# Turning x by VectorE's 32x32 squares and transfers, and loading mixing's x behind its store

## The chip, the cores and the metric

The kernel runs on one core of a Trainium2 chip. The metric is the device time of one execution in microseconds. Every engine of the core (TensorE for matmuls, VectorE, ScalarE and GpSimd for the rest, SyncE for starting transfers) has its own queue of instructions and works through it in order. They wait for each other by semaphores.

## The reference

A graph network of four layers works on x of 8 batches, 2048 nodes and 64 features. Each layer adds its result to x and normalizes over the features.

```python
# layer 0: hypergraph attention; "industry" and "g" are mixed with two weights per node
industry = einsum('nm,bmf->bnf', adj / deg, x @ W_ind)
g        = einsum('bne,benf->bnf', coefs1, all_he)
coefs2   = softmax(attn_scores(stack([industry, g], 2)), -1)      # "mixing"
x = layernorm(x + einsum('bnk,bnkf->bnf', coefs2, pair))
# layer 1: x = layernorm(x + (A_hat @ x) @ W.T)
# layer 2: supports I, adj, 2*adj@adj - I, softmax(relu(E @ E.T)); weights per node
x_g = einsum('knm,bmc->bknc', supports, x)
out = einsum('bnki,nkio->bno', x_g, einsum('nd,dkio->nkio', emb, weights_pool)) + bias
# layer 3: three steps of v -> W2 @ relu(W1 @ [v, adj @ v] + b1) + b2
for _ in range(3):
    h = relu(einsum('bnk,dk->bnd', concat([v, adj @ v]), W1) + b1)
    v = einsum('bnk,dk->bnd', h, W2) + b2
```

## The kernel before

Batches are handled in pairs (p = 0 to 3), so that two batches' 64 features fill 128 partitions. The nodes lie in 16 tiles of 128, or in 4 chunks (c) of 512. adj stays in SBUF. The big products (`u`) go through TensorE in the order of the program. A "filler" generator supplies their matmuls between other work; `fill(n)` takes n of them. After each of them `tick()` counts down what `later(n, f)` and `after(n, f)` have put off. The list of `later` is served strictly in its order: an entry that is due waits for those ahead of it. On the other engines a scheduler decides the order of most instructions when the kernel is built; those wrapped in `pin` keep the order of the program.

Mixing of step i (pair and chunk) loads g, turns it for TensorE, loads x into `r` (two buffers) and adds g to it on GpSimd:

```python
def mix_g(i):
    p, c = divmod(i, NCH)
    gn = mp.tile([P, JT, P], F32, tag="gn", name="gn", bufs=2)
    nc.sync.dma_start(gn, gs_hbm...)                      # cut
    rs[i] = mp.tile([P, JT, P], F32, tag="r", name="r", bufs=2)
    load_x(rs[i], p, c)
    pg = lps.tile([P, C], F32, tag="mm", name="pg", bufs=4)
    for j in range(JT):
        transpose(pg[:, cols(j, P)], gn[:, j, :])
    gts[i] = mp.tile([P, C], F32, tag="gt", name="gt", bufs=2)
    pin(nc.scalar.activation(gts[i], pg, AF.Identity, bias=-1.0))
    r = rs[i]
    after(8, lambda: pin(nc.gpsimd.tensor_tensor(r, r, gn, ALU.add)))

def mix_scores(i):
    # cut: four matmuls pf, four tanh on ScalarE
    pin(nc.gpsimd.tensor_tensor(inds[i], inds[i], gts[i], ALU.subtract))
    after(5, differences)

def mix_end(i):
    # cut: pt <- transposes of inds[i]
    def end():
        nc.sync.dma_start(x1_hbm[p][:, wide(c), :], r)    # frees the buffer r
        # cut
    after(3, add_up, 0, *normalized(mp, r, r, False, end))

for i in range(steps + 1):
    k = 9 if i > NCH else 8
    if i < steps:
        mix_scores(i); fill(k)
    if i > 0:
        mix_end(i - 1); fill(k)
    if i + 1 < steps:
        mix_load(i + 2); mix_ind(i + 1); mix_g(i + 1); fill(k)
    if i < steps:
        mix_weigh(i); fill(k)
```

Layer 2 needs x turned (features on the partitions) in DRAM, to be loaded as a part of `xg`. Each chunk is turned while u1 = adj @ x is made:

```python
def out_t(hbm, c, src, eng):
    ut = va.tile([P, C], F32, tag="ut", name="ut", bufs=2)
    # cut: copy src (PSUM) to ut by ScalarE or VectorE
    nc.sync.dma_start(hbm[:, cols(c)], ut)

def natural(c, ut):
    pn = lps.tile([P, JT, P], F32, tag="mm", name="pn", bufs=4)
    for j in range(JT):
        transpose(pn[:, j, :], ut[:, cols(j, P)])
    x_part[c] = split(va, pn, f"v{c}", 1, [P, JT, P])

def turned_x(p, c):
    pt = lps.tile([P, C], F32, tag="mm", name="pt", bufs=4)
    for j in range(JT):
        transpose(pt[:, cols(j, P)], xn[p][:, c * JT + j, :])
    out_t(xt_hbm[p], c, pt, nc.scalar)
    # cut: xn += bias on GpSimd

# in supports(): k = 1 is u1 = adj @ x, k = 2 is u2 = adj @ u1, each in two halves g
if k == 1 and g == 0:
    turned_x(p, q)                       # after each chunk q of the first half
if k == 1 and g == 1 and q in uts:
    natural(q, uts.pop(q))               # u1 of the first half, turned back for k = 2

def load_xg(p, c, b):
    until(p, 2, c // 2)
    a, z = (l2.tile([P, C], F32, tag=f"g{2 * b + q}", name=f"xg{b}{q}") for q in range(2))
    # cut: four transfers from xt_hbm, u1_hbm, u2_hbm, u3_hbm into halves of a and z
```

Layer 2's products with the weights (`py`) follow for each pair and chunk, with `fill(2)` between them; VectorE multiplies each by the embeddings and sums it up. Layer 3 needs x turned in SBUF, as `h`:

```python
def first_h(p, c, h):
    pt = lps.tile([P, C], F32, tag="mm", name="pt", bufs=4)
    for j in range(JT):
        transpose(pt[:, cols(j, P)], xn[p][:, c * JT + j, :])
    nc.scalar.copy(h, pt)
    if c == 0:
        nc.vector.tensor_copy(h[:, 0:1], ivc)
    return h

def first(c, n):
    h[c] = first_h(0, c, l2.tile([P, C], F32, tag=f"g{c}", name=f"h{c}"))
    later(n, lambda: factor(c, h[c], bd_e, None))   # factor: matmuls pr, then the split into v0h, v0l, ...

# layer 3, for each pair p, step and half g (cut)
if last and p + 1 < NP:
    for c in own:
        def prepare(c=c):
            h_next[c] = first_h(p + 1, c, new_h(c))
        later(2 if g else 40, prepare)
# ... in g == 1 of the last step: later(3, factor(c, h_next[c], ...)) for c = 0 to 2, and c = 3 at its end
# ... and of the half before: later(14 + 8 * k, finish(p, c, h)): po, layernorm, out_x <- r
```

A `check` at several t of each half loads a piece of adj into `fcav` and compares it.

Of the kernel before, what the change touches and what calls it, by code (L numbers as in the profile page):

```python
# [30 lines left out]
F32 = mybir.dt.float32  # L31
# [6 lines left out]
ALU = mybir.AluOpType  # L38
# [18 lines left out]
def tile_gnn_fast(  # L57
# [265 lines left out]
    def products():  # L323

        deg1 = hy.tile([P, NT], F32, name="deg1")

        def degrees(g):
            du = pph.tile([P, 2, C], F32, tag="ph", name=f"du{g}", bufs=2)
            for t in range(NT):
                for i in range(2):  # L330
                    mm(
                        du[:, i, :], lhsT=ones_r, rhs=adj_c(t, 2 * g + i), start=t == 0, stop=t == NT - 1
                    )
                    yield
            for i in range(2):
                c = 2 * g + i
                r = slice(c * P // NCH, (c + 1) * P // NCH)
                evacuate(deg4[r, :], du[r, i, :])

        def inverses():  # L340

            pdc = places["small"]([P, JT, P], "pdc")
            for j in range(JT):
                transpose(pdc[:, j, :], deg4[:, cols(j, P)])
            pdc = pdc.rearrange("p j (c r) -> p c j r", c=NCH)[:, :, :, 0]
            d1 = deg1.rearrange("p (c j) -> p c j", c=NCH)
            nc.vector.tensor_scalar(d1, pdc, 1.0, None, op0=ALU.add)
            nc.gpsimd.tensor_tensor(dinv, deg1, neg_half[:, :NT], ALU.pow)
            nc.vector.tensor_scalar(d1, pdc, 1.0, None, op0=ALU.max)
            nc.vector.reciprocal(deg1, deg1)  # L350
            for _ in range(8):
                yield
            for c in range(NCH):
                pt = places["small"]([P, C], "pinv")
                for j in range(JT):
                    k = c * JT + j
                    transpose(pt[:, cols(j, P)], deg1[:, k:k + 1].to_broadcast([P, P]))
                row = va.tile([P, C], F32, tag="ut", name="inv", bufs=2)
                nc.scalar.copy(row, pt)
                nc.sync.dma_start(inv_hbm[:, cols(c)], row)  # L360
                for _ in range(4):
                    yield

        for p in range(NP):
            for g in range(2):
                own = (2 * g, 2 * g + 1)
                ug = pph.tile([P, 2, C], F32, tag="ph", name="ug", bufs=2)
                u = {c: ug[:, c % 2, :] for c in own}
                turning = inverses() if p == 0 and g == 1 else iter(())
                for t in range(NT):  # L370
                    for i in range(2):
                        for c in own:
                            mm(
                                u[c], lhsT=part[t // JT][i][:, t % JT, :], rhs=adj_c(t, c),
                                start=t == 0 and i == 0, stop=t == NT - 1 and i == 1,
                            )
                            tick()
                            if t > 1:
                                next(turning, None)
                            yield  # L380
                    if p == NP - 1 and g == 1 and t % JT == JT - 1:
                        first_parts(t // JT, free)
                    if p + 1 < NP and t % JT == JT - 1:
                        c = t // JT
                        if g == 1:
                            parts(p + 1, c)
                        if g == 1 and c < 2 or g == 0 and c >= 2:
                            fetch(p + 1, (c + 2) % NCH)
                if p == NP - 1:

                    for t in range(g * NT // 2, (g + 1) * NT // 2):
                        onto_diagonal(t, nc.gpsimd, ALU.add)
                for c in own:
                    ut = va.tile([P, C], F32, tag="ut", name="ut", bufs=2)
                    nc.scalar.copy(ut, u[c])
                    nc.sync.dma_start(u0_hbm[p][:, cols(c)], ut)
                if p == 0 and g == 0:
                    yield from degrees(0)
                    yield from degrees(1)
# [412 lines left out]
    def wide(c):  # L812
        return slice(c * JT, (c + 1) * JT)

    uts, invs, gts, inds, tts, rs = {}, {}, {}, {}, {}, {}
    xn, done, stored, due = [], [0] * NP, set(), set()


# [49 lines left out]
# [4 lines that stand above are left out]
        nc.sync.dma_start(  # L872
            gn, gs_hbm.rearrange("(p t) f -> p t f", t=NT)[:, wide(c), p * P:(p + 1) * P]
        )
        rs[i] = mp.tile([P, JT, P], F32, tag="r", name="r", bufs=2)
        load_x(rs[i], p, c)
        pg = lps.tile([P, C], F32, tag="mm", name="pg", bufs=4)
        for j in range(JT):
            transpose(pg[:, cols(j, P)], gn[:, j, :])
        gts[i] = mp.tile([P, C], F32, tag="gt", name="gt", bufs=2)  # L880
        pin(nc.scalar.activation(gts[i], pg, AF.Identity, bias=-1.0))
        r = rs[i]
        after(8, lambda: pin(nc.gpsimd.tensor_tensor(r, r, gn, ALU.add)))

    def mix_scores(i):

        t1 = []
        for src in (inds[i], gts[i]):
            for b in range(2):

                s = slice(b * F, (b + 1) * F)
                pf = lps.tile([P, C], F32, tag="mm", name="pf", bufs=4)
                mm(pf, lhsT=fc2[s, :], rhs=src[s, :], start=True, stop=True)
                t1.append(mp.tile([P, C], F32, tag="t1", name="t1", bufs=4))
                pin(nc.scalar.activation(t1[-1], pf, AF.Tanh, bias=fcb_col))
        tts[i] = t1[0:2]

        def differences():
            for b in range(2):
                pin(nc.vector.tensor_tensor(t1[b], t1[b], t1[2 + b], ALU.subtract))  # L900

        pin(nc.gpsimd.tensor_tensor(inds[i], inds[i], gts[i], ALU.subtract))
        after(5, differences)

    def mix_weigh(i):

# [10 lines left out]
    def mix_end(i):  # L917
        p, c = divmod(i, NCH)
        r = rs.pop(i)
        pt = lps.tile([P, C], F32, tag="mm", name="pt", bufs=4)  # L920
        for j in range(JT):
            transpose(pt[:, cols(j, P)], inds[i][:, cols(j, P)])

        def end():
            nc.sync.dma_start(x1_hbm[p][:, wide(c), :], r)
            stored.add((p, c))
            if p == 0:
                first_parts(c, mixed)
            elif (p, c) in due:
                l1_parts(p, c)  # L930

        def add_up():
            pin(nc.vector.scalar_tensor_tensor(
                r, pt.rearrange("p (t f) -> p t f", f=P), 0.5, r, op0=ALU.mult, op1=ALU.add
            ))

        after(3, add_up, 0, *normalized(mp, r, r, False, end))
# [85 lines left out]
    mix_load(1)  # L1023
    fill(24)
    mix_ind(0)
    fill(12)
    mix_g(0)
    fill(4)
    for i in range(steps + 1):
        k = 9 if i > NCH else 8  # L1030
# [162 lines left out]
    def natural(c, ut):  # L1193
# [3 lines left out]
            transpose(pn[:, j, :], ut[:, cols(j, P)])  # L1197
        x_part[c] = split(va, pn, f"v{c}", 1, [P, JT, P])

    def turned_x(p, c):  # L1200
        pt = lps.tile([P, C], F32, tag="mm", name="pt", bufs=4)
        for j in range(JT):
            transpose(pt[:, cols(j, P)], xn[p][:, c * JT + j, :])
        out_t(xt_hbm[p], c, pt, nc.scalar)

        bias = l2.tile([P, JT, 1, F], F32, tag="bias", name="bias", bufs=1)
        nc.sync.dma_start(bias[:, :, 0, :], bias_hbm[:, wide(c), :])
        x4 = xn[p][:, wide(c), :].rearrange("p t (b f) -> p t b f", f=F)
        nc.gpsimd.tensor_tensor(x4, x4, bias.to_broadcast([P, JT, 2, F]), ALU.add)
# [88 lines left out]

    def first_h(p, c, h):

        pt = lps.tile([P, C], F32, tag="mm", name="pt", bufs=4)
        for j in range(JT):
            transpose(pt[:, cols(j, P)], xn[p][:, c * JT + j, :])
        nc.scalar.copy(h, pt)
        if c == 0:

            nc.vector.tensor_copy(h[:, 0:1], ivc)
        return h
# [21 lines left out]
    for p in range(NP):  # L1330
        for c in range(NCH):
            r = staged("r").rearrange("p t (b f) -> p t b f", f=F)
            for b in range(2):
                a_z = xg[b]
                for j in range(JT):
                    e_b = emb_n[:, c * JT + j:c * JT + j + 1, :].to_broadcast([P, OH, D])
                    for k in range(2):
# [5 lines left out]
                        nc.vector.tensor_tensor(pr, py, e_b, ALU.mult)  # L1343
                        nc.vector.tensor_reduce(r[:, j, b, cols(k, OH)], pr, AX.X, ALU.add)  # L1344
                        fill(2)
                    if p == NP - 1 and c == NCH - 1 and b == 1 and j in (1, 2):

                        first(j - 1, 2)
                if c + 1 < NCH:
                    load_xg(p, c + 1, b)  # L1350
                elif p + 1 < NP:
# [9 lines left out]

    STEPS = 3
    for c in (2, 3):
        first(c, 4 * c)
    bd_v2 = l2.tile([P, P], F32, name="bd_v2")
    rows = l2.tile([P, 2, P], F32, tag="e", name="rows")
    more = l2.tile([P, 2, P], F32, tag="bias", name="more")
# [888 lines left out]
```

## Time and profile before

| | |
|---|---|
| time, median of 3 runs | 1966.11 us (1965.88 to 1972.42) |
| span of the profiled execution | 1961.8 us |
| mixing | about 240 to 500 us |
| softmax support of layer 2 (`ua`) | about 546 to 786 us |
| supports and weights of layer 2 | about 786 to 1482 us |
| layer 3 | about 1483 to 1962 us |
| `pt<-ident,xn` | 128 transposes, 789.7 to 1819.8 us, 272 ns each from start to end |
| `r<-in_x_n` | 16 transfers of 256 KB, 2.7 us to landing |
| VectorE, ScalarE, GpSimd busy | 51%, 20%, 27% |

The page has the busy time of each engine, the chain of work that ended last, and the groups of instructions; the trace can be asked for the waits of one engine and for stretches of time. PE is TensorE, PEld its loads of weights, DVE VectorE, ACT ScalarE, POOL GpSimd, SPq SyncE's queue, in which transfers are issued. In `pt<-ident,xn` the name before the arrow is written and those behind it are read. Matmuls overlap, so what one costs is read from the distance between starts and not from its duration.

### The profile page before, as it was taken

How to read it: one execution, taken by the hardware profiler on the slowest of the kernel's cores; microseconds unless marked ns; L12 is line 12 of the kernel's file. 1: busy time of each engine (PE TensorE's matmuls, PEld its weight loads, DVE VectorE, ACT ScalarE, POOL GpSimd, SP SyncE). 2: the span in 40 equal slices, each digit the busy share in tenths (PEclk: the TensorE clock that was granted, in tenths of full speed). 3: DMA queues.
4: the chain of work that ended last, by engine and by line, in shares of the span. 5: the costliest groups of instructions: out<-in, count | busy, mean ns of one | idle time of the engine just before them, and what ended most of it. 6: DMA issues, size and time to landing. Idle time of an engine off the chain costs nothing.

```text
span 1961.8 us, 19565 instructions
## 1 busy us (share of the span) xinstructions
PE 1867.9 (95%) x7100; PEld 1211.1 (62%) x7100; DVE 1004.3 (51%) x1741; ACT 392.7 (20%) x771; POOL 529.5 (27%) x480
## 2 busy tenths in 40 slices
PE   6888899888899999999999999999999999999997
PEld 4666565555754444855665575566547787877875
DVE  7789555565532211356556736754785343343332
ACT  1455343333222121100000000000002121222211
POOL 3678644454454434311001101100001020100201
PEclk9999899999999999999999999999999999999999
DMA  9923333432500000311101111111111122121211
GB/s 322 308 87 107 121 129 126 127 118 80 175 6 27 25 3 22 119 38 60 48 33 43 57 52 33 46 57 35 43 33 35 43 55 54 44 54 49 54 27 24
DMA packets 94185, 143.10 MB, mean 73 GB/s; under 512 B 29232, under 2 KB 40112, under 8 KB 93696
## 3 DMA queue, kind: packets, MB, share of 16 engines
q1 hardware_dynamic: 83920, 105.39, 17.7%
q0 software_dynamic: 7760, 27.66, 4.2%
q10 hardware_dynamic: 2400, 8.72, 1.2%
q8 instruction: 58, 0.95, 0.2%
q14 instruction: 47, 0.39, 0.1%
HBM read 98.67 MB, written 43.06 MB: 72 GB/s over the span
## 4 chain that ended last, share of the span: by engine, by line
PE 76%; DMA 4%; POOL 3%; DVE 3%; issue 2%; ACT 1%; SPq 0%; POOLq 0%; ACTq 0%; DVEq 0%
PE u L171 34%; PE py L171 22%; PE ua L171 11%; PE pr L171 2%; PE ug L171 2%; POOL ln_r L843 1%; DMA x_hbm<-r 1%; PE po L171 1%; DMA r<-in_x_n 1%; PE pf L171 1%; PE pt L174 1%; PE s L171 1%; DVE r L846 0%; DMA gs_hbm<-acc,order 0%; POOL r L968 0%
## 5 line engine op out<-in xcount | busy, mean ns | idle before, releaser
L171 PE MATMUL py<-wp,xg 128*128 128x512 f32 x1024 | 475.2, 592 | 0.7 <-DMA xg<-u_hbm 0.7
L171 PEld LDWEIGHTS py<-wp,xg 128*128 128x128 f32 x1024 | 193.3, 189 | 161.4 <-issue 138.8
L1343 DVE TENSOR_TENSOR fcav<-py,emb_n 128x512 f32<-128x512 f32 x256 | 176.9, 691 | 135.0 <-PE py L171 129.1
L171 PE MATMUL ua<-pt,xn 128*128 128x512 f32 x512 | 230.2, 592 | 1.5 <-DVE pt L1124 1.5
L1344 DVE TENSOR_REDUCE r<-fcav 128x32 f32<-128x512 f32 x256 | 175.5, 686 | 8.2
L171 PEld LDWEIGHTS ua<-pt,xn 128*128 128x128 f32 x512 | 96.9, 190 | 111.2 <-issue 104.2
L154 POOL TENSOR_TENSOR ln_r<-ln_e,neg_half 128x8 f32<-128x8 f32 x32 | 53.5, 1671 | 399.4 <-DVE ln_e L152 370.0
L171 PE MATMUL u<-adj,v0h 128*128 128x512 f32 x384 | 147.7, 452 | 1.3 <-ACT h L1499 1.3
L171 PE MATMUL u<-adj,v2l 128*128 128x512 f32 x384 | 141.0, 432 | 1.3 <-DVE v2l L167 1.3
L171 PE MATMUL u<-adj,v2h 128*128 128x512 f32 x384 | 141.3, 434 | 0.0
L171 PE MATMUL u<-adj,v1h 128*128 128x512 f32 x384 | 140.8, 434 | 0.0
L171 PE MATMUL u<-adj,v0l 128*128 128x512 f32 x384 | 139.8, 431 | 0.0
L171 PE MATMUL u<-adj,v3l 128*128 128x512 f32 x384 | 138.9, 426 | 0.0
L171 PE MATMUL u<-adj,v1l 128*128 128x512 f32 x384 | 138.4, 427 | 0.0
L171 PE MATMUL u<-adj,v3h 128*128 128x512 f32 x384 | 138.4, 427 | 0.0
L1124 DVE TENSOR_SCALAR pt<-pt 128x512 f32<-128x512 f32 x64 | 30.3, 473 | 150.5 <-ACT pt L1123 150.3
L1130 POOL TENSOR_TENSOR acc<-acc,pt 128x512 f32<-128x512 f32 x60 | 76.5, 1275 | 107.0 <-DVE pt L1124 106.4
L1425 DVE SCALAR_TENSOR_TENSOR ar<-fcav,ar 128x512 f32<-128x512 f32 x64 | 46.8, 731 | 108.7 <-ACT ar L1424 108.7
L171 PEld LDWEIGHTS u<-adj,v0h 128*128 128x128 f32 x384 | 71.0, 189 | 36.7 <-issue 24.1
L171 PEld LDWEIGHTS u<-adj,v2l 128*128 128x128 f32 x384 | 72.8, 191 | 31.9 <-issue 15.9
L171 PEld LDWEIGHTS u<-adj,v1l 128*128 128x128 f32 x384 | 72.9, 190 | 29.3 <-issue 14.4
L171 PEld LDWEIGHTS u<-adj,v3l 128*128 128x128 f32 x384 | 72.1, 188 | 29.4 <-issue 14.9
(360 smaller groups left out, 2717.2 us busy)
## 6 DMA issues: line engine op xcount, KB each, us to landing
adj<-in_adj_t POOLq DMA_DIRECT2D x32, 512.0 KB, 8.0
fcav<-in_adj_t SPq DMA_DIRECT2D x64, 256.0 KB, 2.9
u_hbm<-ut SPq DMA_DIRECT2D x48, 256.0 KB, 2.8
xg<-u_hbm SPq DMA_DIRECT2D x96, 128.0 KB, 2.9
x_hbm<-r SPq DMA_DIRECT2D x28, 256.0 KB, 2.2
hs_hbm<-st ACTq DMA_DIRECT2D x8, 584.0 KB, 5.4
xt<-in_x_t SPq DMA_DIRECT2D x16, 256.0 KB, 6.1
ut<-u_hbm SPq DMA_DIRECT2D x16, 256.0 KB, 3.4
```

The lines of the kernel that those rows point to most:

```text
L154: nc.gpsimd.tensor_tensor(rstd, vare, neg_half[:, :groups], ALU.pow)
L171: tc.keep_in_program_order(nc.tensor.matmul(*args, **kw))
L174: tc.keep_in_program_order(nc.tensor.transpose(dst, src, ident))
L843: pin(nc.gpsimd.tensor_tensor(rstd, vare, neg_half[:, :groups], ALU.pow))
L1124: nc.vector.tensor_scalar(pt, pt, 1.0, None, op0=ALU.max)
L1130: nc.gpsimd.tensor_tensor(accs[c], accs[c], pt, ALU.add)
L1343: nc.vector.tensor_tensor(pr, py, e_b, ALU.mult)
L1344: nc.vector.tensor_reduce(r[:, j, b, cols(k, OH)], pr, AX.X, ALU.add)
L1425: nc.vector.scalar_tensor_tensor(ar.bitcast(F32), seen_a, 1.0, ar.bitcast(F32), op0=ALU.mult, op1=ALU.not_equal, accum_out=left[:, t, k:k ...
```

## The change

Two things are changed. First, x of layers 2 and 3 is no longer turned by TensorE: VectorE transposes the 32x32 squares of a 128x512 tile, each in its place, and 16 transfers carry the squares to where they belong, to DRAM in layer 2 and to SBUF in layer 3. It is meant to take the transposes and their evacuations from TensorE, PSUM and ScalarE. The distances of `first` are set anew for it. Second, mixing's x is asked for behind the store that frees its buffer, and g is added to it later in the step, behind ind - gt, so that GpSimd should not stand waiting. The rows of inverse degrees are turned some matmuls later.

```diff
@@ inverses
-            for _ in range(8):
+            for _ in range(20):
                 yield
@@ mix_g
-        rs[i] = mp.tile([P, JT, P], F32, tag="r", name="r", bufs=2)
-        load_x(rs[i], p, c)
+        gns[i] = gn
...
-        r = rs[i]
-        after(8, lambda: pin(nc.gpsimd.tensor_tensor(r, r, gn, ALU.add)))
+
+    def mix_x(i):
+        if i < steps:
+            rs[i] = mp.tile([P, JT, P], F32, tag="r", name="r", bufs=2)
+            load_x(rs[i], *divmod(i, NCH))
@@ mix_scores
         after(5, differences)
+        r, gn = rs[i], gns.pop(i)
+        after(8, lambda: pin(nc.gpsimd.tensor_tensor(r, r, gn, ALU.add)))
@@ mix_end
             nc.sync.dma_start(x1_hbm[p][:, wide(c), :], r)
+            mix_x(i + 2)
@@ before the loop
     mix_ind(0)
-    fill(12)
+    fill(28)
     mix_g(0)
+    mix_x(0)
+    mix_x(1)
     fill(4)
@@ layer 2
+    def turn(p, c, dst):
+        S = 32
+        squares = va.tile([P, C], F32, tag="ut", name="squares", bufs=2)
+        nc.vector.transpose(squares, xn[p][:, wide(c), :].rearrange("p t f -> p (t f)"))
+        dst = dst.rearrange("(m r) (j i q) -> i m r j q", r=S, i=P // S, q=S)
+        for i in range(P // S):
+            src = squares[i * S:(i + 1) * S, :].rearrange("r (j m q) -> m r j q", j=JT, q=S)
+            for m in range(P // S):
+                nc.sync.dma_start(dst[i, m], src[m])
+
     def turned_x(p, c):
-        pt = lps.tile([P, C], F32, tag="mm", name="pt", bufs=4)
-        for j in range(JT):
-            transpose(pt[:, cols(j, P)], xn[p][:, c * JT + j, :])
-        out_t(xt_hbm[p], c, pt, nc.scalar)
+        turn(p, c, xt_hbm[p][:, cols(c)])
@@ first_h
-        pt = lps.tile([P, C], F32, tag="mm", name="pt", bufs=4)
-        for j in range(JT):
-            transpose(pt[:, cols(j, P)], xn[p][:, c * JT + j, :])
-        nc.scalar.copy(h, pt)
+        turn(p, c, h)
@@ the last chunk of layer 2
-                    if p == NP - 1 and c == NCH - 1 and b == 1 and j in (1, 2):
-                        first(j - 1, 2)
+                    if p == NP - 1 and c == NCH - 1 and b == 1 and j == 0:
+                        first(0, 5)
+                        first(1, 6)
@@ layer 3
     for c in (2, 3):
-        first(c, 4 * c)
+        first(c, 10 + 5 * c)
```

## What the kernel should do after the change

> **What bounds the kernel now.** I read the page's busy times and its chain first, then the waits of single engines, then busy time by stretches, then timelines around the places that the diff touches. The first part of the page gives TensorE's matmuls 95% of the span, and its chain agrees:
>
> ```profile
> PE 1867.9 (95%) x7100; PEld 1211.1 (62%) x7100; DVE 1004.3 (51%) x1741; ACT 392.7 (20%) x771; POOL 529.5 (27%) x480
> ...
> PE 76%; DMA 4%; POOL 3%; DVE 3%; issue 2%; ACT 1%; SPq 0%; POOLq 0%; ACTq 0%; DVEq 0%
> ```
>
> So time is won by taking work from TensorE or by closing its gaps, and lost by opening one. The table by stretches (columns: length, busy time of PE, PEld, DVE, ACT, POOL, then granted clock) shows the gaps of mixing:
>
> ```profile
> 300.00:350.00 50.00, 47.19 (x200) 29.61 (x199) 23.40 (x37) 18.05 (x33) 21.42 (x21) 0.97 0.39 125
> 350.00:400.00 50.00, 42.35 (x188) 28.39 (x187) 30.21 (x42) 14.72 (x26) 28.12 (x20) 0.93 0.38 119
> 400.00:450.00 50.00, 40.53 (x183) 26.76 (x181) 28.07 (x42) 17.15 (x30) 21.91 (x16) 0.97 0.36 113
> 450.00:500.00 50.00, 45.28 (x184) 29.57 (x184) 31.43 (x51) 14.23 (x25) 26.55 (x19) 0.97 0.26 85
> ```
>
> The reader is to see 2.8 + 7.7 + 9.5 + 4.7 = 24.7 us without a matmul, and a clock that sags with it. From 545 to 1830 us TensorE is idle for under 4 us. Who holds mixing up is in GpSimd's waits (columns: us, times, longest), over 240 to 545 us:
>
> ```profile
> POOL r L883 <- DMA r<-in_x_n: 71.3, 12, 7.0
> ```
>
> GpSimd stands in front of r + gn until x has come, 71 us in all, and everything behind it in its queue stands too: ind - gt, the powers, layer 1's sums.
>
> **What the Trainium skill says.** "Vector Engine (DVE) Microarchitecture Reference", section 3.8, says that VectorE's 32x32 transpose is pipelined at one element per cycle and lane. A 128x512 tile should then cost what the other 512-column passes here cost, 0.69 us; no transposition on VectorE is in this trace. "DMA: Bandwidth & Descriptors", Rules for kernel authors, says that transfers under 64 KB pay mostly overhead. The new ones have 16 KB. The trace agrees: six transfers of 64 single numbers each took SyncE 0.59 us apiece, the 128 KB xg loads 0.44 to 0.57 us. "TensorE: Matmul & The Clock Gate", Why this matters for your kernels, warns that an idle gap of some 3 us drops the clock. The trace agrees: the stretch 370:380 has 2.79 us of matmul and a clock of 0.76, the next one 0.90.
>
> **The change part by part.** *TensorE's transposes.* There are 16 turns in layer 2 and 16 in layer 3, each of four transposes. One turn in the timeline:
>
> ```profile
> 789.28 0.62 PE L171 MATMUL u<-adj,v2l 128*128 128x512 f32 x2
> 789.74 0.60 PE L174 MATMUL pt<-ident,xn 128*128 128x128 f32 x4
> 790.10 0.72 PE L171 MATMUL u<-adj,v3h 128*128 128x512 f32 x2
> 790.65 0.62 PE L171 MATMUL u<-adj,v3l 128*128 128x512 f32 x2
> ```
>
> A pair of matmuls takes 0.465 us undisturbed. From 789.74 to 790.65 a pair and a turn take 0.91, so a turn costs 0.44 us: 32 x 0.44 = 14 us saved, all on the bound engine.
>
> *Mixing.* The load of x keeps its dependence on the store (2.1 us + 2.7 us), but GpSimd's addition moves from 8 ticks after mix_g to 8 after mix_scores, behind ind - gt. This should take most of the 71 us from GpSimd. TensorE's loss from 300 to 545 us is 30 us idle and, from ten-us stretches with a clock under 1, another 10. Not all hangs on this load (5.8 us is from 500 to 545, where the embedding is loaded), so I take half: 20 us. Starting mixing 16 matmuls later only shifts filler.
>
> *The inverses' rows.* Twelve ticks more should remove one wait of TensorE of 2.9 us; VectorE is nearly full there, so 2 us.
>
> *What is added.* A turn now is one pass of VectorE (32 x 0.7 = 22 us beside other work, as VectorE is at 51%) and 16 transfers on SyncE: 512 in all. SyncE's issue is the term that decides. 128-partition transfers took 0.32 us, 64-partition ones 0.44 to 0.59. For 32 partitions I choose 0.5: 8 us a turn, and 2 us until the last has landed. Before, a result was there about 1 us after the matmuls. I followed the compiled order of each engine for three places.
>
> *(a) Start of layer 2.* SyncE's timeline before:
>
> ```profile
> 797.13 1.13 SPq L115 DMA_DIRECT2D bd_v<-in_w_t  x2
> 798.35 1.18 SPq L115 DMA_DIRECT2D bd_e<-in_w_t  x2
> 799.58 2.51 SPq L122 DMA_DIRECT2D few<-in_b  x4
> 802.13 1.24 SPq L122 DMA_DIRECT2D few<-in_iv  x2
> ```
>
> The four turns of pair 0 stand behind these, so they are issued from 803.4 to about 837 us, with a bias load (0.4) after each. The squares share the two buffers "ut" with the evacuations of u: the first must wait until the third turn has landed (830), the second until the fourth (839). The transposes of u1 (pn) stood at 813.9 and 818.1 us; now they can start near 831 and 839.5. No other work is ready for TensorE. Loss: 19 + 4 = 23 us.
>
> *(b) Layer 2 to layer 3.* The first turn goes out when the b=0 half of the last chunk is done, the four follow each other 8 us apart, and VectorE's write of column 0 waits for the first to land. With factor at ticks 5, 6, 20 and 25, I get waits of 2.3, 1.4, 1.8 and 5.9 us: 11 us.
>
> *(c) Layer 3, between pairs.* The turns of chunks 2 and 3 stand on SyncE behind the stores of the previous pair's chunks 0 and 1, which wait for their layernorm. Before:
>
> ```profile
> 1590.55 0.95 SPq L1406 DMA_DIRECT2D out_x<-r  x2
> 1593.81 0.35 SPq L1419 DMA_DIRECT2D fcav<-in_adj_t  x1
> 1596.04 0.92 SPq L1406 DMA_DIRECT2D out_x<-r  x2
> ```
>
> and TensorE wants chunk 2 at:
>
> ```profile
> 1597.05 1.05 PE L171 MATMUL pr<-bd_e,h 128*128 128x128 f32 x8
> ```
>
> In the new order the second store goes out near 1598; turn 2 is issued from 1599 to 1607 and lands at 1609, turn 3 at 1617. TensorE, now 0.9 us earlier at 1596, waits 12.6 us, and 4.1 us more before chunk 3: 17 us, at three changes of pair, 50 us.
>
> Within layer 2 the turns of pairs 1 to 3 fill SyncE for 64 x 0.5 = 32 us in some 147 and an xg load has some 16 us from release to use: nothing lost.
>
> Idle gaps of this length also lower the clock: about 8 us for the seven or so of them.
>
> Sum: -14 - 20 - 2 + 23 + 11 + 50 + 8 = +56 us.
>
> **Rivals.** First, cheap issue: if a transfer costs 0.33 us like one of 128 partitions, (a) is 13, (b) 5, (c) about 34, clock 5, and the sum is +21 us. The 0.37 to 0.40 us of the three-dimensional stores of out_x speaks for it, the 64-partition loads against it. Second, the gain wins: mixing returns all 40 us and TensorE its 14, and the new waits stay small, because the ticks were chosen for that; then 1925 to 1960. Against it, turn 2 in (c) follows a store at 1596 even in the old timeline, and 16 x 0.33 + 2 us later is after 1597 by any count. Third, issue dearer than I think: 0.65 us or more, when many 128-byte pieces back up; then (a) 32, (b) 20, (c) 65, and layer 2's loads begin to be late: +90 us or above.
>
> **Range and chances.** Between +21 at 0.33 us and +56 at 0.5 us lies a straight line of some 2 us per hundredth: 0.33, 0.45, 0.55 and 0.65 us give +21, +46, +66 and +90. Weighed with 25, 25, 35 and 15% the mean is +53; a little less for the chance that mixing gains more than half. From 1966 this is 2015 us; 8 in 10 between 1962 and 2062. Faster than 1927 needs every gain and hardly a new wait: 5%. Slower than 2005 begins at an issue of about 0.45 us: 60%. The rest, 35%, within 2%.
>
> **What would show it.** Right: the addition r + gn no longer waits tens of us for x; TensorE waits for the turned tiles' transfers or for VectorE's copies behind them near the start of layer 2 and at each change of pair in layer 3, in gaps of over 5 us; SyncE's transfers from the squares take about 0.5 us each, back to back; the stretches of mixing have under 15 us idle. Wrong: no transfer of the squares in the chain and TensorE above 96% in layers 2 and 3 (cheap issue, or slack that I overlooked), or gaps all through layer 2 (dearer issue).

## The result, and the profile after

The changed kernel takes 2053.2 us (median; 2051.5 to 2058.2) against 1966.0 us of the kernel before beside it: a ratio of 1.045, with a 95% interval of 1.041 to 1.048. It is 87 us slower. The prediction was 2015 us, with a range of 1962 to 2062.

First the page of the kernel after, its busy times and its chain:

```profile
PE 1875.6 (91%) x6972; PEld 1214.1 (59%) x6972; DVE 1021.1 (50%) x1773; ACT 376.9 (18%) x739; POOL 528.5 (26%) x480
...
PE 16%; SPq 6%; DMA 1%; DVE 1%; issue 1%; POOL 1%; ACT 0%; POOLq 0%; ACTq 0%; DVEq 0%
```

TensorE falls from 95% to 91% and SyncE's issue of transfers (SPq) stands in the chain with 6%. This chain can be followed back only to 1510 us, so its shares add up to 26% and can't be set beside those of before: of the 546 us that it covers, SyncE's issue of squares takes some 113. TensorE's busy time itself doesn't fall, though 128 transposes are gone: a part of the matmuls has become longer, where the clock is lower (below).

Four points of the trace cut the span into stages: the first `ua` matmul, the first and the last `py` matmul, the end. (us)

| profile of | to first ua | to first py | to last py | to the end | span |
|---|---|---|---|---|---|
| before | 546.7 | 292.5 | 642.1 | 480.5 | 1961.8 |
| after | 519.3 | 314.6 | 635.9 | 586.6 | 2056.4 |
| difference | -27.4 | +22.1 | -6.2 | +106.1 | +94.6 |

The change wins in mixing and in the long middle of layer 2, and loses at the start of layer 2 and above all in layer 3, its border included.

Mixing, by stretches as before (length, then busy time of PE, PEld, DVE, ACT, POOL, then the clock):

```profile
300.00:350.00 50.00, 50.00 (x224) 32.19 (x223) 31.58 (x46) 20.71 (x36) 28.95 (x26) 1.00 0.45 146
350.00:400.00 50.00, 49.32 (x227) 33.27 (x227) 36.15 (x49) 19.31 (x34) 29.57 (x22) 1.00 0.44 141
400.00:450.00 50.00, 50.00 (x230) 33.13 (x229) 39.37 (x57) 20.75 (x36) 30.91 (x22) 1.00 0.39 127
450.00:500.00 50.00, 42.27 (x178) 31.85 (x177) 31.38 (x51) 13.92 (x25) 22.29 (x15) 0.86 0.49 169
```

From 300 to 450 us TensorE now lacks 0.7 us instead of 19.9, at full clock. Of the 7.7 us of the last row, 3.6 are a wait for the end of mixing (`pt` for `ind`) and 4.1 one for the embedding, and its clock is lower than before, 0.86 against 0.97. GpSimd's wait for x, 71.3 us before, is down to:

```profile
POOL r L907 <- DMA r<-in_x_n: 25.1, 9, 4.6
```

That is a third, but still tens of us, which the prediction had expected to be gone. TensorE's waits from 500 us on show the price (us, times, longest):

```profile
PE pr L171 <- DMA h<-squares: 89.5, 12, 18.4
PE pn L174 <- ACT ut L1192: 16.9, 1, 16.9
PE pn L174 <- DVE ut L1194: 3.1, 1, 3.1
```

And the cost of one transfer stands in the instructions of the squares (duration in ns: lowest, median, highest):

```profile
L1216 SPq DMA_DIRECT2D xt_hbm<-squares x256: 312/430/1784, 776.0 to 1272.0; - x128
L1216 SPq DMA_DIRECT2D h<-squares x256: 585/599/1662, 1455.0 to 1923.5; - x128
L1211 DVE STREAM_TRANSPOSE squares<-xn x32: 689/703/712, 770.3 to 1898.1; 128x512 f32<-128x512 f32 x32
```

Sixteen in a row into DRAM take 7.65 us, 0.48 each. Into SBUF 64 in a row take 42.36 us, 0.66 each:

```profile
776.01 7.65 SPq L1216 DMA_DIRECT2D xt_hbm<-squares  x16
1454.95 42.36 SPq L1216 DMA_DIRECT2D h<-squares  x64
```

VectorE's pass costs the 0.7 us that the Trainium skill, "Vector Engine (DVE) Microarchitecture Reference", section 3.8, led to.

Now one change of pair in layer 3, in SyncE's timeline (start, length, transfers, number):

```profile
1580.99 19.36 SPq L1216 DMA_DIRECT2D h<-squares  x30
1600.45 4.80 SPq L1432 DMA_DIRECT2D fcav<-in_adj_t  x2
1608.24 4.56 SPq L1419 DMA_DIRECT2D out_x<-r  x4
1612.90 21.45 SPq L1216 DMA_DIRECT2D h<-squares  x32
```

The first row is the end of the turns of chunks 0 and 1, the last is the turns of chunks 2 and 3. TensorE waits 1.70, 18.39 and 5.18 us for them, 25.3 in all. For 12.6 us, from 1600.35 to 1612.90, SyncE issues no square. What the waits do to TensorE is in the stretches (same columns as above):

```profile
1600.00:1610.00 10.00, 4.87 (x24) 3.82 (x24) 3.44 (x8) 2.26 (x4) 3.21 (x2) 1.00 0.31 73
1610.00:1620.00 10.00, 0.00 (x0) 0.00 (x0) 2.94 (x3) 0.00 (x0) 2.56 (x3) 0.56 0.25 50
1620.00:1630.00 10.00, 5.08 (x19) 4.50 (x20) 1.39 (x3) 1.20 (x2) 0.00 (x0) 0.58 0.16 26
1630.00:1640.00 10.00, 4.82 (x14) 3.07 (x13) 2.49 (x6) 1.79 (x3) 0.00 (x0) 0.76 0.20 41
1640.00:1650.00 10.00, 10.00 (x47) 7.86 (x46) 3.01 (x9) 1.25 (x2) 1.65 (x1) 0.90 0.22 52
```

The clock is 0.56 to 0.76 for 30 us. The chain shows the same in the matmuls `u`, the first right behind the gap:

```profile
1637.88 6.58 PE u L171 x16
...
1648.12 15.71 PE u L171 x64
```

That is 0.41 us a matmul against 0.25 ten us later. What the lower clock costs can be estimated from such ten-us stretches: TensorE's busy time in each, times what the clock lacks to 1 (from 1620 to 1630 us: 5.08 x 0.42 = 2.1 us). From the first point of each stage on, idle time and this estimate add up to (us):

| profile of | layer 2's start: idle, clock | layer 3: idle, clock |
|---|---|---|
| before | 0.0, 0.0 | 15.9, 0.0 |
| after | 20.0, 3.6 | 105.9, 18.4 |
| early (below) | 21.0, 3.3 | 57.2, 17.0 |

So some 22 us of the loss are matmuls at a lower clock, and no wait shows them.

### The profile page after: what moved, and what is told of

Read it like the earlier page. It is cut to its first block, busy times and chain, and to the rows that moved or that the text cites. A ratio compares the mean times of both kernels' runs of the same rounds, so it can differ in the third digit from the quotient of the medians.

```text
span 2056.4 us, 20022 instructions
## 1 busy us (share of the span) xinstructions
PE 1875.6 (91%) x6972; PEld 1214.1 (59%) x6972; DVE 1021.1 (50%) x1773; ACT 376.9 (18%) x739; POOL 528.5 (26%) x480
## 5 line engine op out<-in xcount | busy, mean ns | idle before, releaser
L171 PE MATMUL pr<-bd_e,h 128*128 128x128 f32 x128 | 25.4, 361 | 89.5 <-DMA h<-squares 89.5
L171 PEld LDWEIGHTS u<-adj,v3h 128*128 128x128 f32 x384 | 74.3, 194 | 30.0 <-issue 15.0
```

The source lines that it names most:

```text
L171: tc.keep_in_program_order(nc.tensor.matmul(*args, **kw))
```

## The experiments

My theory: mixing is a gain by itself. The loss is the serial issue of 16 transfers a turn, wherever TensorE has no other work. The rivals put it down to the 128-byte packets, to the buffers that the squares share, or to the clock; or they say that mixing's gain is paid back.

| run | ratio, 95% interval | to ua | to py | py | to the end |
|---|---|---|---|---|---|
| mix_only | 0.985 (0.983 to 0.987) | 514.6 | 292.5 | 642.0 | 481.7 |
| turns_only | 1.059 (1.057 to 1.061) | 551.9 | 314.1 | 636.1 | 589.2 |
| layer2_turns | 0.994 (0.992 to 0.996) | 518.5 | 314.9 | 636.8 | 481.2 |
| two_queues | 1.000 (0.999 to 1.001) | 518.5 | 302.8 | 636.0 | 509.0 |
| own_squares | 1.045 (1.043 to 1.047) | 513.6 | 314.4 | 636.1 | 588.1 |
| stores_aside | 1.037 (1.035 to 1.039) | 517.2 | 312.8 | 636.0 | 572.9 |
| early | 1.016 (1.015 to 1.018) | 511.9 | 315.2 | 636.0 | 535.4 |
| own_early | 1.018 (1.017 to 1.020) | 516.7 | 314.9 | 636.0 | 532.9 |
| mix_again | 0.985 (0.983 to 0.986) | 518.0 | 292.5 | 642.0 | 481.7 |
| mix_inv8 | 0.985 (0.983 to 0.986) | 516.1 | 292.5 | 641.9 | 483.5 |
| later_pairs | 0.983 (0.982 to 0.985) | 513.5 | 292.5 | 636.7 | 482.4 |
| slack_only | 0.993 (0.992 to 0.995) | 517.1 | 293.5 | 636.7 | 506.2 |

The first column spreads by several us between kernels that are alike up to there (511.9 to 519.3 in those with the new mixing). The others repeat to about 2 us, so small effects are read from them.

**The parts alone: mix_only.** The turns go back to TensorE, with the old distances of `first`:

```diff
-        turn(p, c, xt_hbm[p][:, cols(c)])
+        pt = lps.tile([P, C], F32, tag="mm", name="pt", bufs=4)
+        for j in range(JT):
+            transpose(pt[:, cols(j, P)], xn[p][:, c * JT + j, :])
+        out_t(xt_hbm[p], c, pt, nc.scalar)
# and in first_h the same four transposes with nc.scalar.copy(h, pt)
```

> Layers 2 and 3 keep TensorE's transposes; only mixing's x behind the store and the inverses' 20 ticks are taken from the change. Theory (the turns are the loss, mixing is a gain of its own): the first ua matmul comes at 519 us as in the changed kernel, and everything after it is as before, so 1966 - 27 = 1939 us, 1933 to 1945. Rival (the earlier work of mixing is paid back later in layers 1 to 3, whatever turns x): the gain at ua is there, but the end is at 1955 or later.

Measured: 1933.4 us. Nothing is paid back: all later stages are within 1.2 us of those before. Mixing alone gains 30 us, and this kernel is faster than both. Which part of it gains is not shown: no run separates the load of x behind the store, the later addition of g and the start of mixing 16 matmuls later.

**turns_only.** Before's mixing and inverses, with the turns of the change:

```diff
-    def mix_x(i): ...
+    # in mix_g, as before: rs[i] = mp.tile(...); load_x(rs[i], p, c); after(8, r + gn)
-            for _ in range(20):
+            for _ in range(8):
```

> Only the turns by VectorE's squares and transfers; mixing and the inverses as before. Theory (the parts add): 2053 + 27 = 2080 us, 2070 to 2090; first ua at 546 us. Rival (part of the loss comes of layer 2 starting with less prepared after the faster mixing): 2060 or less.

Measured: 2079.6 us, the theory's number. -1.5% and +5.9% add up to +4.3%, and the whole change is +4.5% (4.1 to 4.8%). There is no sign that the parts act on each other.

**layer2_turns.** Only `first_h` goes back to TensorE, with the old distances of `first`:

```diff
-        turn(p, c, h)
+        # in first_h: four transposes into pt, nc.scalar.copy(h, pt)
```

> As the changed kernel, but layer 3's sixteen turns by TensorE again. Theory (layer 3 loses 106 us to the turns that stand in SyncE's queue): 2053 - 106 = 1947 us, 1940 to 1956, with the 17 us wait at the start of layer 2 still there and no wait of pr for h above 2 us. Rival (the slower layer 3 has its cause in the lower clock or in what layer 2 leaves behind): above 1975.

Measured: 1952.6 us, in the theory's range. Layer 3 and its border cost 5.1%, some 100 us, and come back to 481.2 us without the squares. The wait at the start of layer 2 stays at 17.4 + 3.1 us.

**two_queues.** The same transfers, half of them issued by ScalarE:

```diff
-                nc.sync.dma_start(dst[i, m], src[m])
+                (nc.scalar if m % 2 else nc.sync).dma_start(dst[i, m], src[m])
```

> As the changed kernel, but every second transfer of a turn is issued by ScalarE instead of SyncE; bytes, packets and buffers are the same. Theory (the serial issue on one engine decides, 0.48 us into DRAM and 0.66 us into SBUF): a turn takes about half as long to issue, the waits of pr for h fall from 89.5 us to 30 to 55, the one at the start of layer 2 from 17 to under 7, and the time to 1975 to 2015; ScalarE's evacuations behind its own transfers may cost a part of that. Rival (the 128-byte packets themselves, on the DMA engines, decide): the waits stay within 15% and the time within 15 us of 2053.

Measured: 1965.7 us, a gain of 88 us, more than either theory gave. This run decides between issue and packets: bytes, packets and buffers are the same, only the queues are two. Each of the two takes as long for a transfer as the one did (median 599 ns in the changed kernel):

```profile
L1216 SPq DMA_DIRECT2D h<-squares x128: 585/600/1925, 1442.5 to 1834.7; - x128
L1216 ACTq DMA_DIRECT2D h<-squares x128: 592/612/1627, 1442.5 to 1832.3; - x128
```

So what one queue does for each transfer is the cost, and the DMA engines behind it took twice as many in the time. TensorE's waits fall to

```profile
PE pr L171 <- DMA h<-squares: 21.4, 4, 8.2
PE pn L174 <- ACT ut L1192: 10.1, 1, 10.1
```

The second is not under 7 us. ScalarE now issues 23 us long before it comes to copy u1. In its timeline:

```profile
770.24 23.05 ACTq L1216 DMA_DIRECT2D xt_hbm<-squares  x32
793.54 0.58 ACT L1192 COPY ut<-u 128x512 f32<-128x512 f32 x1 [35.82 <-DMA bias<-bias_hbm]
```

The issue ends at 793.29 and the copy follows at 793.54. But the copy also needs the buffer of the third turn, whose half on SyncE's queue is issued until 791.54 and lands some 1.5 us later, so what it waited for last isn't settled.

**own_squares.** The squares of pair 0 in layer 2 get tiles of their own:

```diff
-        squares = va.tile([P, C], F32, tag="ut", name="squares", bufs=2)
+        place = (l2, f"g{c}", 1) if own else (va, "ut", 2)     # own: p == 0 in layer 2
+        squares = place[0].tile([P, C], F32, tag=place[1], name="squares", bufs=place[2])
```

> As the changed kernel, but in layer 2 the squares of pair 0 lie in four tiles that are still empty then (g0 to g3), not in the two ut buffers that the evacuations of u1 need; SyncE issues the same transfers at the same times. Theory (what TensorE waits for at the start of layer 2 is the buffer, not the data): the waits of pn for ut, 16.9 + 3.1 us, fall under 2 us in all, and with the clock that sags in the gap the time falls by 20 to 28 us, to 2025 to 2033. Rival (SyncE's queue itself holds layer 2 up, since u1's stores and the bias loads stand in it behind the turns): the gap moves but stays, 2045 or more.

Measured: 2057.0 us, ratio 1.045 as after. The theory, and with it a step of my prediction, falls; it is the rival's picture. u1 is made in two halves of two chunks, and ScalarE copies one chunk of each. Its timeline:

```profile
768.10 0.59 ACT L1192 COPY ut<-u 128x512 f32<-128x512 f32 x1 [15.24 <-PE u L171]
...
806.73 0.58 ACT L1192 COPY ut<-u 128x512 f32<-128x512 f32 x1 [22.22 <-DMA u_hbm<-ut]
```

The first goes out at once, at 768 instead of 801 us. But the second needs its buffer again, and the store that frees it stands behind all four turns. SyncE:

```profile
795.76 7.49 SPq L1217 DMA_DIRECT2D xt_hbm<-squares  x16
803.36 0.37 SPq L1223 DMA_DIRECT2D bias<-bias_hbm  x1
804.13 0.81 SPq L1195 DMA_DIRECT2D u_hbm<-ut  x2
```

One wait of 22.1 us takes the place of 16.9 + 3.1. It is the queue, with or without the squares in the shared buffers.

**stores_aside.** The stores of out_x leave SyncE's queue:

```diff
-            (nc.scalar if b and p == NP - 1 and c == NCH - 1 else nc.sync).dma_start(   # out_x <- r
+            (nc.scalar if b and p == NP - 1 and c == NCH - 1 else nc.gpsimd).dma_start(
```

> As the changed kernel, but the stores of out_x go out on GpSimd's queue. Theory as predicted (the turns of chunks 2 and 3 stand on SyncE behind stores that wait for their layernorm): those turns begin where the turns of chunks 0 and 1 end, some 8 to 12 us sooner, and each change of pair waits 10 to 17 us instead of 25: 2005 to 2030. Rival (64 transfers of 0.66 us are simply more than one engine can issue in the time, whatever stands between them): the waits of pr for h stay above 75 of 89.5 us and the time above 2040.

Measured: 2040.9 us, 12 less than after (ratio 1.037 against 1.045), and 76.3 us of waits for h: outside the theory's 2005 to 2030 and just inside the rival's bounds (2040 and 75). The stores are some 4 us of each change of pair, not the heart of it. With them gone VectorE's timeline shows what holds the turns of chunks 2 and 3:

```profile
1601.28 0.69 DVE L1438 SCALAR_TENSOR_TENSOR ar<-fcav,ar 128x512 f32<-128x512 f32 x1 [6.52 <-ACT ar L1437]
...
1605.29 1.29 DVE L1211 STREAM_TRANSPOSE squares<-xn 128x512 f32<-128x512 f32 x2
```

and SyncE's, where the turns follow at once:

```profile
1578.00 19.37 SPq L1216 DMA_DIRECT2D h<-squares  x30
1597.47 4.87 SPq L1432 DMA_DIRECT2D fcav<-in_adj_t  x2
1606.07 21.47 SPq L1216 DMA_DIRECT2D h<-squares  x32
```

I read a ring from this: the turns of chunks 0 and 1 hold the queue to 1597 us, behind them comes the load for the check of adj, for it ScalarE waits (cast `ar`, 6.60 us, until 1600.63) with the layernorm behind the cast, VectorE waits for ScalarE, and VectorE's passes for chunks 2 and 3 stand behind that. No run takes a single link out of it, and there is a second link of nearly the same length. `ar`, the layernorm and the squares share the two buffers "ut". The squares of chunk 1 are issued until 1597.37 and land in some 1.8 us, so their buffer comes free only a good us before the load has landed. In the changed kernel the cast waits for squares as well (us, times, longest):

```profile
ACT ar L1437 <- DMA h<-squares: 67.0, 6, 19.9
```

Both links end with the issue of the first two turns.

**early.** The turns of the next pair begin a step sooner, ahead of all stores:

```diff
-                        later(2 if g else 40, prepare)           # in the last step
+                            if step == STEPS - 2 and p + 1 < NP:  # behind each factor of the step before
+                                later(at + 2, prepare)
```

> As the changed kernel, but in layer 3 the turns of the next pair begin a step earlier, each after the factor of its chunk at the end of step 2 of 3, so that they are issued through the whole last step and ahead of all out_x stores. Theory (nothing but the late start of 42 us of issue is exposed at a change of pair): there pr no longer waits for h (under 3 us each time), 17 us stay at the border of layers 2 and 3, and the time falls by 70 to 90 us, to 1963 to 1985; the loads of the adjacency check stand behind the turns instead and may hold ScalarE up, which is the larger part of that range. Rival (the half clock and the 128-byte packets cost TensorE time even where nothing waits): above 2000 with few waits left.

Measured: 2000.2 us, 53 less than after; the expected 70 to 90 were too many, and the time stands at the rival's bound of 2000. But the rival had few waits left, and here TensorE still has these (us, times, longest):

```profile
PE pr L171 <- DMA h<-squares: 17.5, 3, 8.1
PE pn L174 <- ACT ut L1192: 17.4, 1, 17.4
PE pr L171 <- ACT h L1506: 13.3, 5, 5.2
PE u L171 <- ACT v3h L166: 10.1, 3, 4.2
```

Where pairs change, TensorE no longer waits for h; the 17.5 us are the border of layers 2 and 3. New are 23 us for ScalarE. Its casts `ar` wait for the check's loads (191 us, 46 times) and for the squares' buffers (57 us, 9 times), and h stands behind such a cast, as at 1638.42 us. These waits are about as long in the changed kernel (184 and 67 us), so their sums don't tell what they cost TensorE. As for the clock, TensorE's idle time in layer 3 falls by 48.7 us, but what the lower clock costs stays, 17.0 us against 18.4 by the table of the stretches. The gaps are now of 2 to 8 us.

**own_early.** Both edits together:

```diff
+        place = (l2, f"g{c}", 1) if own else (va, "ut", 2)
+                                later(at + 2, prepare)
```

> Both of the last: squares of pair 0 in their own tiles and the turns of layer 3 a step earlier. Theory (the gaps add, and behind them lie the 14 us of TensorE's transposes as the change meant): what is left is the border of layers 2 and 3, about 17 us and its clock, so 1936 to 1958. Rival (the queue of SyncE is so full in layers 2 and 3 that one gap closed opens another): above 1970.

Measured: 2004.7 us, as early within the intervals, so the rival's side: own tiles do as little here as alone, with one wait of 22.5 us at the start of layer 2.

**mix_again.** The diff of mix_only, as a base for three more.

> The kernel of mix_only once more, as the base for the three that follow on the same chip: 1933 us, within 4 us, by every theory.

Measured: 1936.6 us, ratio 0.985 again.

**mix_inv8.** The inverses as before:

```diff
-            for _ in range(20):
+            for _ in range(8):
```

> As mix_only, but the inverses wait 8 ticks as before instead of 20. Theory (the inverses' rows were worth 2 us and mixing's x the other 30): 1933 to 1938 us. Rival (the ticks have a good part in the 32 us): 1941 or more.

Measured: 1935.8 us, ratio 0.985 as mix_again. The inverses' ticks are worth nothing that can be measured.

**later_pairs.** mix_only, with squares in layer 2 for pairs 1 to 3 only:

```diff
+        if p > 0:
+            turn(p, c, xt_hbm[p][:, cols(c)])
+        else:
             # four transposes into pt, out_t(xt_hbm[p], c, pt, nc.scalar)
```

> As mix_only, but x of pairs 1 to 3 of layer 2 is turned by VectorE's squares and SyncE's transfers; pair 0 and layer 3 stay with TensorE. Theory (where nothing is exposed, the change pays what it was meant to: 12 turns of 0.44 us): 5 us less than mix_only, 1926 to 1930. Rival (192 transfers and VectorE's passes between the py work cost as much as they save): within 2 us of mix_only or slower.

Measured: 1932.0 us, ratio 0.983 against 0.985: the intervals overlap, so the whole time doesn't settle 5 us. The stage does. First mix_again's `py`, then that of later_pairs (last two times: first and last start):

```profile
L171 PE MATMUL py<-wp,xg x1024: 592/592/667, 810.5 to 1452.5; 128*128 128x512 f32 x171
```

```profile
L171 PE MATMUL py<-wp,xg x1024: 592/592/668, 806.0 to 1442.7; 128*128 128x512 f32 x171
```

642.0 against 636.7 us: 5.3 us for 12 turns, 0.44 each.

**slack_only.** later_pairs and early for layer 3's pairs 1 to 3, with the check's loads on GpSimd's queue:

```diff
-        nc.sync.dma_start(seen_a, adj_t[t * P:(t + 1) * P, cols(k)])
+        nc.gpsimd.dma_start(seen_a, adj_t[t * P:(t + 1) * P, cols(k)])
```

> As later_pairs, and layer 3's pairs 1 to 3 by squares too, begun a step earlier, with the loads of the adjacency check on GpSimd's queue so that they don't stand behind the turns; the border of layers 2 and 3 stays with TensorE. Theory (in the run with early turns what was left between the pairs was ScalarE standing behind those loads, 23 us in the waits of pr and u for ScalarE): these waits fall under 4 us and 24 turns of 0.44 us are saved, 10 us less than mix_only, 1920 to 1928. Rival (squares in layer 3 cost something beside the queue, in the clock or in the order of the engines): above mix_only.

Measured: 1954.2 us, slower than mix_again. The rival holds, by 24 us in the last stage. TensorE no longer waits for a transfer into h at all, but 16.2 + 2.1 us (po and pr) for the h that ScalarE writes, and by the ten-us stretches 7.8 us are lower clock. ScalarE's own waits say why the loads' queue was not enough:

```profile
ACT ar L1448 <- DMA fcav<-in_adj_t: 198.4, 48, 10.2
ACT ar L1448 <- DMA h<-squares: 64.7, 9, 8.5
```

The first was 170.8 us in mix_again, and the second wasn't there. The cast `ar` takes one of the two buffers "ut", which the squares hold until their last transfer has landed. I read this from the waits; a run with squares of their own in layer 3 was not made, so how much of the 24 us it is stays open.

## Why the prediction was right, and where its steps were not

The range and the likeliest outcome (slower by over 2%) held, and so did the mechanism: TensorE waits for what SyncE issues one transfer after another, at the three places that were named. The size was not as good. The result is 38 us above the predicted 2015 and lies near the case "issue dearer than I think" (+90 us), to which the prediction gave 15%. It is 9 us inside the range, and mixing's larger gain is 7 of them. By steps:

- **TensorE's transposes, -14.** Right where it can be seen: 5.3 us for 12 turns in later_pairs is 0.44 each. For layer 3's turns no run shows it alone. That nothing is lost within layer 2 is right too: the py stage is 6.2 us shorter.
- **Mixing, -20.** Mis-sized. "I take half" was wrong of the idle time: nearly all of it from 300 to 450 us went. The 10 us for the clock were too many: they took the ten-us stretches whole, idle time included, and with busy time alone are 7.4. Of the -27.4 in the profile 23.1 are idle time and 2.8 clock. mix_only has -30.
- **The inverses, -2.** Nothing (mix_inv8).
- **Issue, 0.5 us a transfer.** 0.48 into DRAM, 0.66 into SBUF. I took one number for two kinds of destination. This is the step that cost most: the prediction's own sums at 0.65 us are 20 for (b) and 65 for (c), near what follows.
- **(a) +23.** The size is right: 16.9 + 3.1 us of waits. Its mechanism is only half of it: the shared buffers are what TensorE waits for, but own_squares shows the same loss from u1's stores in SyncE's queue.
- **(b) +11.** 17.1 us (7.07 + 1.96 + 8.05).
- **(c) +50.** 72.4 us (89.5 - 17.1), 24 at each change of pair. The order was as predicted, the turns of chunks 2 and 3 behind the stores. But the reason given, that they wait for these stores, fails: stores_aside gives only 12 us in all to the stores. By the timelines it was ScalarE and VectorE, held by the check's load and the buffers until the first two turns were out; two_queues shows that the issue is the cause.
- **The clock, +8.** Too small: 3.6 + 18.4 = 22 us by the stretches, an estimate, as no run changed the clock alone. The Trainium skill, "TensorE: Matmul & The Clock Gate", Why this matters for your kernels, has the warning; I had priced the gaps and not the work behind them.

The sum of these terms is -27.4 - 14.1 + 20.0 + 89.5 + 22.0 = +90, and the profiles differ by 94.6; some 5 us stay open. Against the prediction (b) is 6 us more, (c) 22 and the clock 14, mixing's gain is 7 more, the inverses' 2 less and (a) 3 less: 56 + 42 - 7 + 2 - 3 = +90.

## What to carry to other kernels

Before giving an engine's work to transfers, count the transfers and multiply by the issue time of their shape and destination in a trace. 16 transfers took 7.7 to 10.6 us of a queue to save 0.44 us of TensorE, which paid only in layer 2, where the result was wanted much later, and in layer 3 not even then (slack_only). Then look at everything else in that queue, since what stands behind a burst (a small load, a store that frees a buffer) can stop engines that have nothing to do with it. And try the parts of a change one by one: here the small part was worth 30 us and the large one cost some 115.

## What was not expected

- The same 16 KB transfer costs its queue 0.48 us into DRAM and 0.66 us into SBUF. Why is not shown.
- Half the issue on each queue left less than a third of the waits (89.5 + 20.0 us to 21.4 + 10.1), and with mixing's gain the kernel is then level with the one before. That fits a gap that opens only by what a burst is longer than the work beside it: it shrinks faster than the burst.
- Taking a wait's cause away moved the wait twice: own tiles for the squares gave 22.1 us for 20.0, and the check's loads on another queue left ScalarE waiting for the buffers.
- Shorter gaps did not bring the clock back: early has 48.7 us less of idle time in layer 3 than the changed kernel, in gaps of 2 to 8 us, and still 17.0 of 18.4 us of lower clock.
